# Two chained attention blocks on one core: the loads, transposes and centring of the first microseconds, and the check of the last ones, put in another order

## Chip, cores and metric

The kernel runs on one core of a Trainium2 chip. The metric is the device time of one execution in microseconds (us). An execution computes everything that the reference computes, from inputs in DRAM to the output in DRAM.

## The reference

The input x has the shape (4, 128, 96, 96) in float32: four images of 128 channels and 9216 pixels. Two layers follow each other, each with its own parameters:

```
g     = maxpool2(conv1x1(x, g_w, g_b))      # 64 channels, 48 x 48 = 2304 keys
theta = conv1x1(x, theta_w, theta_b)        # 64 channels, 9216 queries
phi   = maxpool2(conv1x1(x, phi_w, phi_b))  # 64 channels, 2304 keys
attn  = softmax(theta^T phi)                # over the 2304 keys, for each image
y     = attn g^T                            # 64 x 9216
out   = batchnorm(conv1x1(y, W_w, W_b)) + x # 128 x 9216
```

## The kernel before

One image in one layer is a *block*. The eight blocks run in the order of `ORDER`, so that a second layer follows its first with another image between them. The 9216 queries of a block are nine *pairs* of 2 x 512 queries (`Pair`). The 2304 keys are 18 tiles of 128, taken two at a time (`KB`), so a pair has nine steps, and the main loop runs over t = 0 to 647, two key tiles a step.

In a step TensorE makes the scores of two key tiles (`scores`, L351: keys on the partitions, 1024 queries on the free axis, in two buffers of the PSUM pool `ps_sc`), ScalarE turns each into exps (L357, with a constant shift in place of the row maximum), VectorE adds the exps up over the key tiles (`add_up`, L364 and L366) for the denominators, and TensorE multiplies the exps of the step before with the values (`values`, L374). Because the softmax takes a constant shift, notes on the sums and their reciprocals are kept in the tile `notes`. At the end `check` reduces them to one number and `result` writes it as a flag (`flag`). Every engine reads the flag, and `general_blocks`, which takes the true maximum, runs if it says that a sum was too large or too small. For these inputs it does not run.

The order of instructions on TensorE, VectorE, ScalarE and SyncE is written out by hand (`manual_schedule`): each engine takes its instructions in the order of the program text, and a framework places the semaphores. DMAs issued from SyncE (SP) and from ScalarE (ACT) go out in the order of the text too, and one that reuses a semaphore waits for the load that had it before.

The start, before the main loop:

- `load_gphi` loads g's and phi's weights of the first layer (32 KB each), one from ACT's queue and one from SP's. `load_x(0, 12)` loads the first image in 12 loads of 384 KB from SP's queue. `load_theta` loads theta's weights and `columns` four short rows (theta's bias, two variances) from ACT's queue.
- `busy` gives TensorE products of the identity with itself into a tile `warm` (L565, pool `ps_av`): five ahead of the transpose of g's and phi's weights (`make_gphi`, L119) and three behind it.
- `pooled(j)` makes two key tiles: products of x with g's and phi's weights (`products`, L244), and a reduction by VectorE that takes the maximum over 2 x 2 pixels (`pool`, L234). An odd j writes to a buffer of `ps_sc`, an even j to another pool.
- Behind `pooled(0)` come two small transposes, theta's weights (`make_theta`) and the four rows (`first_cols`), each into a buffer of `ps_sc`, and each copied out by VectorE (L121).
- `centring` computes the mean of the first 256 keys, and `batch(j)` has ScalarE subtract it from two key tiles (`centred`, L287) and copy them to the other 64 partitions (`copied`, L293).
- `FIRST` = 6 such batches come ahead of the main loop. The other three are made in its first steps (L208 has their products, in four quadrants of the array). `square` has VectorE transpose the values (L304).

The end: for the last pair `last_denominators` sums the exps by products (L391), takes reciprocals (L399) and has ScalarE sum them up for the notes (L411). `finish` multiplies the values by the reciprocals (L489, four operations of VectorE), makes the last projection (L496), calls `check` (L702 to L708), adds shift and x (L507, four operations), each with its output load (L510), and calls `result` (L712) between the second and the third of them.

Of the kernel before, what the change touches and what calls it, by code (L numbers as in the profile page):

```python
# [9 lines left out]
F32 = mybir.dt.float32  # L10
I32 = mybir.dt.int32
AF = mybir.ActivationFunctionType
ALU = mybir.AluOpType
AX = mybir.AxisListType
PSUM = bass.MemoryType.PSUM

P = 128
# [3 lines left out]
QT = 512  # L21
# [11 lines left out]
PT = 2 * QT  # L33
# [3 lines left out]
FIRST = 6  # L37
# [12 lines left out]
SUM_MIN, SUM_MAX = 1e-20, 1e30  # L50
# [3 lines left out]
def shifted_blocks(ctx: ExitStack, tc: tile.TileContext, x: bass.AP, layers, out: bass.AP, flag):  # L54
# [24 lines left out]
    nc = tc.nc  # L79

    const = ctx.enter_context(tc.tile_pool(name="const", bufs=1))
# [4 lines left out]
    ps_sc = ctx.enter_context(tc.tile_pool(name="ps_sc", bufs=2, space=PSUM))  # L86
# [13 lines left out]
    ones = const.tile([P, CI], F32, name="ones")  # L100
    nc.vector.memset(ones, 1.0)

    notes = const.tile([P, len(ORDER) * NP + 1, 2], F32, name="notes")
    nc.vector.memset(notes, 0.0)

    def load_x(b, n=6):
        xt = xp.tile([C, HW], F32, tag="x", name=f"x_{b}")
        src = x[b].rearrange("c h w -> c (h w)")
        for i in range(n):
            nc.sync.dma_start(out=xt[:, ts(i, HW // n)], in_=src[:, ts(i, HW // n)])  # L110
        return xt
# [86 lines left out]
    def two_banks(name):  # L198
        return [ps_misc.tile([P, QT], F32, tag="misc", name=f"{name}_{i}") for i in range(2)]
# [108 lines left out]
    class Pair:  # L308
# [173 lines left out]
        def finish(self, check, result):  # L482

            n = QT // 2
            y = work.tile([P, PT], F32, tag="halves", name=f"halves_{self.name}")
            for i in range(2):
                for r in range(2):
                    part = slice(r * QT + i * n, r * QT + (i + 1) * n)
                    nc.vector.tensor_mul(y[:, part], self.av[:, part], self.rc[:, ts(i, n)])  # L489
            last = ps_sc.tile([P, PT], F32, tag="sc", name=f"W_ps_{self.name}")  # L490
            pss = [two_banks(f"W_ps_{self.name}"), [last[:, ts(h, QT)] for h in range(2)]]
            for i in range(2):
                for c in range(2):
                    for r in range(2):
                        for h in range(2):
                            nc.tensor.matmul(  # L496
                                pss[i][h][ts(c, CI), :n],
                                lhsT=self.blk.w.W[ts(h, CI), ts(c, CI)],
                                rhs=y[ts(h, CI), r * QT + i * n : r * QT + (i + 1) * n],
                                start=r == 0, stop=r == 1,  # L500
                            )
            good = check()
            for i in range(2):
                for h in range(2):
                    first = (2 * self.p + h) * QT + i * n
                    dst = self.blk.xt[:, first : first + n]
                    nc.vector.scalar_tensor_tensor(  # L507
                        dst, pss[i][h][:, :n], self.blk.w.shift, dst, op0=ALU.add, op1=ALU.add
                    )
                    nc.sync.dma_start(out=self.blk.store[:, first : first + n], in_=dst)  # L510
                if i == 0:
                    result(good)

    def thetas(both):
        pss = two_banks(f"theta_ps_{both[0].name}")
# [12 lines left out]
        return crosswise(part, take)  # L528

    ws = [Layer(l, p) for l, p in enumerate(layers)]  # L530
    ws[0].load_gphi((nc.scalar, nc.sync))
    xs = {0: load_x(0, 12)}
    ws[0].load_theta(nc.scalar)
    first_cols = columns(
        [(ws[0], "theta_b"), (ws[0], "bn_var"), (ws[1], "bn_var")], "first", nc.scalar
    )
# [15 lines left out]
    def begin(n):  # L552

        blocks[n].xt = xs[ORDER[n][0]]
        blocks[n].begin_keys()
# [5 lines left out]
    warm = ps_av.tile([P, PT], F32, tag="av", name="warm_ps")  # L561
# [7 lines left out]
    b0 = blocks[0]  # L569
# [1 line left out]
    ws[0].make_gphi()  # L571
    busy(WARM[1])
    b0.pooled(0)
    ws[0].make_theta(ps_sc.tile([P, PT], F32, tag="sc", name="thetaT_ps")[:, :QT])
    first_cols(ps_sc.tile([P, PT], F32, tag="sc", name="cols_first_ps")[:, :QT])
    b0.centring(KB)
    b0.batch(0)
    for j in range(1, FIRST):
        b0.pooled(j)
        if j == 3:  # L580
            th = ps_sc.tile([P, PT], F32, tag="sc", name="theta_ps_0")[:, :QT]
            pairs[0].theta(th)
            pairs[0].take_theta(th)
        b0.batch(j)
        if j == 1:
            for w in ws:
                w.make_std()
            nc.scalar.preload_act_table(AF.Exp)
# [13 lines left out]
    for n in range(1, len(blocks)):  # L602
        cycle = (n - 1) * NP * NB // CYCLE * CYCLE
        for j in range(NB):
            t = cycle + KEYS[j % len(KEYS)] + j // len(KEYS) * CYCLE
# [13 lines left out]
    for t in range(total + 1):  # L619
        q, s = 2 * (t // CYCLE), t % CYCLE  # L620
        even, odd = pairs[q : q + 2] if t < total else (None, None)
        first, second, take = None, *pending
        pending = (None, None)
        if t in keys:
            n, i = keys[t]
            if n and i == 0:
                begin(n)
            first, *pending = blocks[n].chunks(i)
        elif t < total and s == (THETAS if q else THETAS + 1):
            if q < late:  # L630
                first, *pending = thetas(pairs[q + 1 : q + 3])
            else:
                first, take = odd.theta_alone()
        elif t == total - 1:
            second, take = even.multiply, even.add
        elif gone and s in PROJECT:
            pair = gone[PROJECT.index(s)]
            second, take = pair.multiply, pair.add
        if t < total:
            now, j = divmod(t, NB)  # L640
            if s == 0 and q:
                gone = pairs[q - 2 : q]
            if t in loads:
                xs[loads[t]] = load_x(loads[t])
        for i in range(KB):
            if t < total:
                pairs[now].scores(j * KB + i)
            if i == 0 and first:
                first()
        if second:  # L650
            second()
        for i in range(KB):
            if t < total:
                pairs[now].add_up(j * KB + i)
            if i == 0 and take:
                take()
        if t - 1 in keys and t < NB:
            b0.batch(keys[t - 1][1])
        if t:
            before, j = divmod(t - 1, NB)  # L660
            for k in ends.get(t, range(j * KB, (j + 1) * KB)):
                pairs[before].values(k)
        if t < total:
            for i, pair in enumerate((even, gone[1] if gone else None)):
                if pair is None:
                    continue
                if s in (TURNS[i], TURNS[i] + 1):
                    pair.turn(s - TURNS[i])
                sooner = q == late and i == 0
                if s == (TURNS[0] + 2 if sooner else HALVES[i]):  # L670
                    pair.add_halves()
                if s == (TURNS[0] + 2 if sooner else INVERT[i]):
                    pair.invert()
            for i, pair in enumerate(gone):
                if s == NORM[i]:
                    pair.normalise()
            if q == late and s == 15:
                even.normalise()
        if t == total - 1:
            odd.last_denominators()  # L680
        if t in centres:
            centres[t].centring(KB)
        for i, k in squares.get(t, []):
            b0.square(i, k)
        for k in range(KT // 32):
            if t - k in spreads:
                blk, i = spreads[t - k]
                if k == 0:
                    blk.centred(ts(i, GT * KT))
                if k == 1:  # L690
                    blk.copied(ts(i, GT * KT))
                blk.square(i, k)
        for step in after.pop(t, []):
            step()
    assert not after

    good = const.tile([P, 3], F32, name="good")

    def check():

        ps = ps_sc.tile([P, PT], F32, tag="sc", name="good_ps")[:1, :1]
        nc.vector.tensor_reduce(good[:, 0:1], notes[:, :, 0], AX.X, ALU.add)  # L702
        nc.vector.tensor_scalar(good[:, 1:2], good[:, 0:1], SUM_MAX, None, ALU.is_le)
        nc.vector.tensor_reduce(good[:, 0:1], notes[:, :, 1], AX.X, ALU.add)
        nc.vector.scalar_tensor_tensor(
            good[:, 2:3], good[:, 0:1], 1.0 / SUM_MIN, good[:, 1:2], op0=ALU.is_le, op1=ALU.mult
        )
        nc.tensor.matmul(ps, lhsT=ones[:, :1], rhs=good[:, 2:3], start=True, stop=True)  # L708
        return ps

    def result(ps):
        nc.vector.tensor_scalar(flag, ps, P - 0.5, None, ALU.is_lt)  # L712

    pairs[-1].finish(check, result)

# [303 lines left out]
```

## Time and profile before

| | |
|---|---|
| median of 4 runs | 2496.14 us (2495.37 to 2497.13) |
| profiled execution | 2495.43 us; span from first to last instruction 2493.1 us |
| instructions in the span | 53372 |
| TensorE clock granted, mean | 0.999 |
| busy: TensorE (PE) | 2482.8 us (100% of the span) |
| busy: VectorE (DVE) | 2133.1 us (86%) |
| busy: ScalarE (ACT) | 1542.5 us (62%) |
| exps, L357 | 1296 of 1113 ns |
| sums of exps, L366 | 1151 of 1223 ns |

How to read it: a row of the timeline gives the start in us from the span's start, the time it took, the engine, the line, the operation with the tiles that it writes and reads, and in brackets how long the engine was idle before it and what released it. Equal instructions that follow each other are merged and counted (x8). SPq and ACTq are the instructions by which SyncE and ScalarE issue DMAs. PEld is TensorE's loading of weights, which runs beside its products. A float32 product stands in the trace as two MATMUL records. In the changed kernel the lines stand three to four lower.

### The profile page before, as it was taken

The page shows a single profiled execution, that of the slowest core. Times are in us where ns is not written, and L with a number is a line of the kernel's source. Part 1 is how long each engine was busy: PE and PEld are TensorE (multiplying, and loading weights), DVE is VectorE, ACT ScalarE, POOL GpSimd, SP SyncE. Part 2 cuts the span into 40 slices and gives each one's busy share as a digit, 9 for nine tenths or more (in the row PEclk, how much of TensorE's full clock was granted, in tenths as well). Part 3 has the DMA queues.
Part 4 walks back from the last instruction along what each step waited for, and adds up shares of the span by engine and source line. Part 5 has one row for each costly group of instructions (what it writes and reads, how often), then busy time and mean ns, then how long its engine had stood idle before and what let it go on. Part 6 is the DMA issues. An engine that isn't in the chain of part 4 may idle for free.

```text
span 2493.1 us, 53372 instructions
## 1 busy us (share of the span) xinstructions
PE 2482.8 (100%) x23058; PEld 897.2 (36%) x23058; DVE 2133.1 (86%) x2684; ACT 1542.5 (62%) x1511; POOL 0.7 (0%) x6
## 2 busy tenths in 40 slices
PE   9999999999999999999999999999999999999998
PEld 4333333333333333333333333333333333333333
DVE  7888888888888888888888888888888888888888
ACT  6566666666666666665666566666666566666665
POOL 0000000000000000000000000000000000000000
PEclk9999999999999999999999999999999999999999
DMA  4113111111121222222112112221111221222222
GB/s 157 7 9 86 10 10 10 7 9 10 10 18 23 27 27 19 18 16 75 10 10 18 24 25 27 22 15 10 9 7 9 18 27 23 26 27 26 27 22 41
DMA packets 26888, 60.43 MB, mean 24 GB/s; under 512 B 8330, under 2 KB 9236, under 8 KB 26644
## 3 DMA queue, kind: packets, MB, share of 16 engines
q1 hardware_dynamic: 26476, 56.88, 20.2%
q8 instruction: 182, 2.98, 0.5%
q14 instruction: 62, 0.51, 0.1%
q10 hardware_dynamic: 168, 0.07, 0.0%
HBM read 19.14 MB, written 18.87 MB: 15 GB/s over the span
## 4 chain that ended last, share of the span: by engine, by line


## 5 line engine op out<-in xcount | busy, mean ns | idle before, releaser
L357 ACT ACTIVATE exp<-sc,nshift 128x1024 f32<-128x1024 f32 x1296 | 1386.1, 1113 | 868.7 <-PE sc L351 867.2
L366 DVE TENSOR_TENSOR sum<-sum,exp 128x1024 f32<-128x1024 f32 x1151 | 1407.8, 1223 | 261.3 <-ACT exp L357 214.2
L351 PE MATMUL sc<-theta,phi 64*64 64x512 f32 x10368 | 1248.5, 589 | 0.8 <-ACT exp L357 0.8
L374 PE MATMUL av<-exp,gT 64*64 64x512 f32 x10368 | 1229.6, 589 | 0.0
L374 PEld LDWEIGHTS av<-exp,gT 64*64 64x64 f32 x10368 | 398.8, 133 | 713.3 <-issue 691.8
L351 PEld LDWEIGHTS sc<-theta,phi 64*64 64x64 f32 x10368 | 398.4, 133 | 713.1 <-issue 687.9
L208 PE MATMUL gphi_ps<-x,gphiT 64*64 64x512 f32 x1056 | 137.3, 589 | 0.0
L234 DVE TENSOR_REDUCE gphi<-gphi_ps 128x128 f32<-128x512 f32 x144 | 92.3, 680 | 30.8 <-PE gphi_ps L208 24.6
L364 DVE TENSOR_TENSOR sum<-exp,exp 128x1024 f32<-128x1024 f32 x72 | 88.2, 1225 | 35.5 <-ACT exp L357 34.7
L381 ACT COPY halves<-av 128x1024 f32<-128x1024 f32 x71 | 71.9, 1012 | 50.2 <-PE av L374 50.2
L423 DVE TENSOR_REDUCE parts<-turned 128x16 f32<-128x512 f32 x142 | 97.5, 687 | 4.9
L422 DVE STREAM_TRANSPOSE turned<-sum 128x512 f32<-128x512 f32 x142 | 100.3, 706 | 1.2
L475 DVE SCALAR_TENSOR_TENSOR x<-W_ps,shift,x 128x512 f32<-128x512 f32 x142 | 99.7, 744 | 0.0
L466 PE MATMUL W_ps<-halves,WT 64*64 64x512 f32 x568 | 73.7, 589 | 0.0
L304 DVE STREAM_TRANSPOSE gT<-gphi 32x192 f32<-32x192 f32 x192 | 70.6, 368 | 3.5
L208 PE MATMUL theta_ps<-x,thetaT 64*64 64x512 f32 x560 | 72.8, 589 | 0.0
L208 PEld LDWEIGHTS gphi_ps<-x,gphiT 64*64 64x64 f32 x1056 | 45.2, 132 | 68.1 <-issue 59.2
L435 DVE STREAM_TRANSPOSE four<-parts 32x32 f32<-32x32 f32 x284 | 56.3, 198 | 2.9
L457 DVE TENSOR_TENSOR halves<-halves 128x512 f32<-128x512 f32 x71 | 48.6, 685 | 0.0
L460 DVE TENSOR_TENSOR halves<-halves 128x512 f32<-128x512 f32 x71 | 48.6, 685 | 0.0
L466 PEld LDWEIGHTS W_ps<-halves,WT 64*64 64x64 f32 x568 | 21.7, 133 | 39.2 <-issue 38.7
L208 PEld LDWEIGHTS theta_ps<-x,thetaT 64*64 64x64 f32 x560 | 21.7, 133 | 38.4 <-issue 29.0
(75 smaller groups left out, 216.2 us busy)
## 6 DMA issues: line engine op xcount, KB each, us to landing
halves<-turned SPq DMA_DIRECT2D x142, 128.0 KB
out_dram<-x SPq DMA_DIRECT2D x35, 512.0 KB
x<-in_x_dram SPq DMA_DIRECT2D x18, 768.0 KB
x<-in_x_dram SPq DMA_DIRECT2D x12, 384.0 KB
turned<-both SPq DMA_DIRECT2D x142, 2.0 KB
out_dram<-x SPq DMA_DIRECT2D x4, 128.0 KB
gphi_nat<-in_L_conv_phi_w_dram SPq DMA_DIRECT2D x2, 32.0 KB
rows_other<-in_L_conv_g_b_dram SPq DMA_DIRECT2D x4, 0.2 KB
```

The lines of the kernel that those rows point to most:

```text
L208: nc.tensor.matmul(out, lhsT=lhsT, rhs=rhs, start=step == 0, stop=step == 1)
L234: nc.vector.tensor_reduce(self.gphi[:, ts(k, KT)].rearrange("p (h w) -> p h w", w=w), ps.rearrange("p (h a w b) -> p h w a b", a=2, b=2, w=w),
L351: nc.tensor.matmul(ps[ts(c, CI), ts(h, QT)], lhsT=self.blk.phi[ts(h, CI), ts(2 * k + c, CI)], rhs=self.th[ts(h, CI), :], start=True, stop= ...
L357: nc.scalar.activation(e, ps, AF.Exp, bias=nshift)
L364: nc.vector.tensor_add(self.sum, self.es[0], e)
L366: nc.vector.tensor_add(self.sum, self.sum, e)
L374: nc.tensor.matmul(self.av[ts(h, CI), ts(r, QT)], lhsT=self.blk.gT[ts(r, CI), k, :], rhs=e[ts(r, CI), ts(h, QT)], start=(k == 0), stop=(k ...
L381: nc.scalar.copy(self.halves, self.av)
L422: nc.vector.transpose(self.turned, self.sum[:, ts(h, QT)])
L423: nc.vector.tensor_reduce(self.parts[:, ts(h, QT // SQ)], self.turned.rearrange("p (b k) -> p b k", k=SQ), AX.X, ALU.add,)
L466: nc.tensor.matmul(self.pss[h][ts(c, CI), :], lhsT=self.blk.w.W[ts(h, CI), ts(c, CI)], rhs=self.y[ts(h, CI), :], start=True, stop=True,)
L475: nc.vector.scalar_tensor_tensor(dst, self.pss[h], self.blk.w.shift, dst, op0=ALU.add, op1=ALU.add)
```

## The change

Four things are put in another order:

1. g's and phi's weights of the first layer are both loaded from ACT's queue, so SP's queue begins with x.
2. The two small transposes at the start write to halves of the second bank of the tile `warm` in place of two buffers of `ps_sc`.
3. The last of the six first batches (`batch(5)`) is no longer ahead of the main loop but in its first step, behind the first two exps.
4. `check` is called ahead of the last multiplications and products, and `result` between them and the additions. `check` has one reduction for both notes and one comparison with a tile `limits` (two columns, set at the start), and two products of one column that add up in PSUM, in place of two reductions, two comparisons and one product.

```diff
     notes = const.tile([P, len(ORDER) * NP + 1, 2], F32, name="notes")
     nc.vector.memset(notes, 0.0)
+    limits = const.tile([P, 2], F32, name="limits")
+    for i, limit in enumerate((SUM_MAX, 1.0 / SUM_MIN)):
+        nc.vector.memset(limits[:, i : i + 1], limit)
...
         def finish(self, check, result):
 
             n = QT // 2
+            good = check()
             y = work.tile([P, PT], F32, tag="halves", name=f"halves_{self.name}")
...
-            good = check()
+            result(good)
             for i in range(2):
                 for h in range(2):
...
                     nc.sync.dma_start(out=self.blk.store[:, first : first + n], in_=dst)
-                if i == 0:
-                    result(good)
...
-    ws[0].load_gphi((nc.scalar, nc.sync))
+    ws[0].load_gphi((nc.scalar, nc.scalar))
     xs = {0: load_x(0, 12)}
...
     b0.pooled(0)
-    ws[0].make_theta(ps_sc.tile([P, PT], F32, tag="sc", name="thetaT_ps")[:, :QT])
-    first_cols(ps_sc.tile([P, PT], F32, tag="sc", name="cols_first_ps")[:, :QT])
+    ws[0].make_theta(warm[:, QT : QT + P])
+    first_cols(warm[:, QT + P :])
     b0.centring(KB)
     b0.batch(0)
...
-        b0.batch(j)
+        if j < FIRST - 1:
+            b0.batch(j)
...
+        if t == 0:
+            b0.batch(FIRST - 1)
         if t - 1 in keys and t < NB:
             b0.batch(keys[t - 1][1])
...
-    good = const.tile([P, 3], F32, name="good")
+    good = const.tile([P, 2], F32, name="good")
 
     def check():
 
         ps = ps_sc.tile([P, PT], F32, tag="sc", name="good_ps")[:1, :1]
-        nc.vector.tensor_reduce(good[:, 0:1], notes[:, :, 0], AX.X, ALU.add)
-        nc.vector.tensor_scalar(good[:, 1:2], good[:, 0:1], SUM_MAX, None, ALU.is_le)
-        nc.vector.tensor_reduce(good[:, 0:1], notes[:, :, 1], AX.X, ALU.add)
-        nc.vector.scalar_tensor_tensor(
-            good[:, 2:3], good[:, 0:1], 1.0 / SUM_MIN, good[:, 1:2], op0=ALU.is_le, op1=ALU.mult
-        )
-        nc.tensor.matmul(ps, lhsT=ones[:, :1], rhs=good[:, 2:3], start=True, stop=True)
+        nc.vector.tensor_reduce(good, notes.rearrange("p n w -> p w n"), AX.X, ALU.add)
+        nc.vector.tensor_tensor(good, good, limits, op=ALU.is_le)
+        for i in range(2):
+            nc.tensor.matmul(
+                ps, lhsT=ones[:, :1], rhs=good[:, i : i + 1], start=i == 0, stop=i == 1
+            )
         return ps
 
     def result(ps):
-        nc.vector.tensor_scalar(flag, ps, P - 0.5, None, ALU.is_lt)
+        nc.vector.tensor_scalar(flag, ps, 2 * P - 0.5, None, ALU.is_lt)
```

## The prediction

> **What bounds the kernel now.** I read the page's busy table first, then the timeline of the first 30 us and of the last 10, then who waited for whom on the DMA queue. The page settles what can be won:
>
> ```profile
> PE 2482.8 (100%) x23058; PEld 897.2 (36%) x23058; DVE 2133.1 (86%) x2684; ACT 1542.5 (62%) x1511; POOL 0.7 (0%) x6
> ```
>
> TensorE is busy for 2482.8 of 2493.1 us. The change touches only the first 25 us and the last 10; the stretch from 28.4 to 2476.0 shows 2447.6 us of TensorE in 2447.6 us, and its instructions stay as they are. So the whole play is in the 10.3 us in which TensorE stood idle. 0.2% of this kernel is 5.0 us, about what a measurement of it can tell from no change.
>
> The start, in order of time (start, duration, engine, line, operation, idle before and its releaser):
>
> ```profile
> 0.74 0.58 SPq L135 DMA_DIRECT2D gphi_nat<-in_L_conv_phi_w_dram  x1
> 0.75 0.57 ACTq L135 DMA_DIRECT2D gphi_nat<-in_L_conv_g_w_dram  x1
> 1.35 0.87 ACTq L139 DMA_DIRECT2D theta_nat<-in_L_conv_theta_w_dram  x1
> 1.37 8.33 SPq L110 DMA_DIRECT2D x<-in_x_dram  x12
> 3.65 0.42 PE L119 MATMUL gphiT_ps<-ident,gphi_nat 128*128 128x128 f32 x1
> 3.87 1.11 PE L565 MATMUL warm_ps<-ident 128*128 128x128 f32 x6
> 5.25 2.02 PE L244 MATMUL gphi_ps<-x,gphiT 128*64 128x512 f32 x8 [0.27 <-DMA x<-in_x_dram]
> 7.21 0.27 PE L119 MATMUL thetaT_ps<-ident,theta_nat 64*128 64x64 f32 x1
> 7.33 0.69 DVE L234 TENSOR_REDUCE gphi<-gphi_ps 128x128 f32<-128x512 f32 x1 [0.26 <-PE gphi_ps L244]
> 7.93 0.21 DVE L121 COPY thetaT<-thetaT_ps 128x64 f32<-128x64 f32 x1
> 8.20 5.37 PE L244 MATMUL gphi_ps<-x,gphiT 128*64 128x512 f32 x24 [0.57 <-DVE thetaT L121]
> ```
>
> The weights' transpose at 3.65 starts straight behind five warming products: the weights cost nothing. The first products wait 0.27 us for x, and the next lot 0.57 us for the copy of theta's transpose. Two rows of the queue's waits price a weight load (waiter, what it waited for, total, times, longest):
>
> ```profile
> SPq L110 <- DMA theta_nat<-in_L_conv_theta_w_dram: 2.2, 1, 2.2
> SPq L110 <- DMA gphi_nat<-in_L_conv_phi_w_dram: 0.3, 1, 0.3
> ```
>
> In the queue's timeline the third x load goes out at 2.75, released by phi's weights: landed 2.0 us after their issue at 0.74, with nothing ahead. The fourth goes out at 5.32, released by theta's: 4.0 us after their issue at 1.35, beside an x load of 384 KB. These are the same 32 KB.
>
> Then the first scores:
>
> ```profile
> 19.24 0.50 ACT L287 ACTIVATE phi<-gphi,centre 64x256 f32<-64x256 f32 x1 [1.38 <-DVE gphi L234]
> 20.20 2.12 ACT L357 ACTIVATE exp<-sc,nshift 128x1024 f32<-128x1024 f32 x2
> 21.37 2.09 PE L351 MATMUL sc<-theta,phi 64*64 64x512 f32 x16 [0.77 <-ACT exp L357]
> 25.41 1.28 DVE L234 TENSOR_REDUCE gphi<-gphi_ps 128x128 f32<-128x512 f32 x2
> 26.71 1.11 PE L208 MATMUL gphi_ps<-x,gphiT 64*64 64x512 f32 x8
> ```
>
> and the end:
>
> ```profile
> 2485.57 0.16 DVE L705 SCALAR_TENSOR_TENSOR good<-good 128x1 f32<-128x1 f32 x1
> 2485.65 0.87 DVE L507 SCALAR_TENSOR_TENSOR x<-W_ps,shift,x 128x256 f32<-128x256 f32 x2
> 2486.15 1.79 SPq L510 DMA_DIRECT2D out_dram<-x  x4
> 2486.43 0.13 DVE L712 TENSOR_SCALAR flag<-good_ps 1x1 int32<-1x1 f32 x1
> 2486.50 0.85 DVE L507 SCALAR_TENSOR_TENSOR x<-W_ps,shift,x 128x256 f32<-128x256 f32 x2
> ```
>
> **The change, part by part.** *x ahead of the weights.* SP's x loads start at 0.74 instead of 1.37, 0.63 us sooner. g's weights still go out at 0.75 on ACT's queue, phi's now behind them at about 1.35, theta's at about 1.95, and all beside x. phi's weights then stand exactly where theta's stood: on ACT's queue, issued at 1.35, with an x load ahead. I take theta's row: landed at 5.3. The ends are 1.35 + 2.0 = 3.35 (nothing ahead) and 6.3 (behind two x loads; the second x load was needed at 6.20, 0.95 after the first at 5.25). From landing to first product: about 0.1 for the release, 0.22 from the transpose to the next instruction (3.65 to 3.87), 1.11 for the warming products queued behind it, which are not moved. So the first product starts at 5.3 + 1.43 = 6.73 instead of 5.25: +1.48. x is there by then, so the second pair follows at its pace of 0.86 instead of 0.95: -0.09. With the early end the weights are in time for 3.65 and the first product is held by the warming products to about 5.0: -0.25. With the late end it is +2.4.
>
> The clock: the sixteen warming matmuls have one shape and last 421 ns in the median and 274 at the shortest; the first ten take 2.50 us and the last six 1.11. TensorE gets faster while these run. With the weights late it stands idle from about 4.1 to 5.4 in the middle of that. If it starts slow again, the first products, 1.72 us of them, could take double: up to +1.7 on top. I leave that out of the sum and put it in the range, since most of the warming (3.65 - 1.36 = 2.3 us) has been done by then.
>
> [...]
>
> [...]
>
> Queues moved past: SP's fourth x load now waits for phi's weights (5.3, as it waited for theta's before), the fifth for theta's, one place later; the products need the fifth chunk only 3.4 us after 8.20. The last bn_var row waits on ACT's queue for the first x load (about 4.6); behind it stands only a table load of 1.28 us, and ACT's first work is at 8.88. If the row came over 1 us after the products it would hold the second small transpose.
>
> *Small transposes in the warming tile.* The two transposes no longer hold buffers of the score pool, so the wait of 0.57 us before 8.20 has lost its reason. But both now write one tile, and in the built program the second waits on VectorE's count for the copy of the first. That copy stands behind the reduction that starts at 7.33 and ends at 8.14 either way; the second transpose (0.22 us, before at 7.41 under that reduction) comes after it, and only then the products. The old wait ends at the same copy, so nothing is gained and 0.2 us is added. Bounds: -0.57 if the wait were free, +0.3.
>
> *Last keys centred behind the first exps.* exp 0 no longer waits for the centring at 19.24 (1.38 idle plus 0.93 of work): it starts near 18.95, and TensorE's 0.77 us wait goes. The centring (0.93) then delays exp 2 and 3 by 0.2, and the values need these only from 28.4. What is late next: the products at 26.71 need buffers freed by the reductions of 25.41, which end at 26.69. That chain on VectorE (17.91: two reductions, eight transposes, sum, two transposes, sum, two reductions) is busy throughout and starts from the same products as before; only its sum at 22.35 waited for an exp (ended 22.32), and the transposes ahead of it end at 22.29. So TensorE comes 0.65 earlier and waits again: -0.05, bounds 0 and -0.65.
>
> *Check of sums.* Four small VectorE operations (0.22, 0.15, 0.23, 0.16) become two, about 0.3 and 0.15, ahead of the four multiplications. They can start when ACT's last sum is read (2482.97) and end near 2483.5; the multiplications started at 2483.46: +0.05. Two tiny TensorE products go ahead of products that wait for the multiplications anyway. The additions at 2485.65 started right behind the old check; their products, the first half of the 2.29 us from 2483.94, were done by about 2485.4, so they start near 2485.5, and the last output load goes out 0.15 sooner. The flag is written near 2485.0 instead of 2486.43. The span ends 6.5 us after the old flag: reading it, branching, landing of the outputs. If the outputs decide, the gain is 0.15; if the flag does, 1.4. I take -0.6, as the outputs are still late but the branches start sooner.
>
> *limits* adds two memsets of about 0.06 us near 1.2, when VectorE is idle until 4.11: nothing; 0.1 without that cover.
>
> **Sum.** +1.4 + 0.2 - 0.05 - 0.6 = +0.95, say +1.0. The profiled execution took 2495.43 us (span 2493.1 and 2.3 around it), 0.7 below the median of 2496.14; with +1.0 it would take 2496.4, and the median goes to 2497.1.
>
> **Rivals.** *Weights not held up* (landed by about 3.7): the start costs nothing, 0.2 for the transposes, -0.6 at the end: 2495.6. For it: 32 KB beside 384 KB; against: theta's row. *All as intended*: first products 0.5 sooner, 0.57, 0.77 and up to 1.4 at the end: -3.0, 2493.1. Against it stand the wait on the copy and VectorE's chain. *Weights behind two x loads, or a slow clock*: +2.4 at the start, or +1.4 and up to 1.7: 2498.1 to 2498.8, both 2499.8. *Slower by over 0.2%*: each microsecond that phi's weights land after about 3.9 is a microsecond lost at the start; a loss of 5.0 net of the 0.6 at the end needs them after 9.3 us, behind the fourth x load, which went out at 5.32: 2501.5. The queue's rows show no wait that long.
>
> **Chances.** The forecast 0.55, weights in time 0.20, two loads or slow clock 0.14, all as intended 0.07, over 5 us slower 0.03, over 5 us faster 0.01 (it would take half of all idle time). So faster by over 0.2% 0.01, within 0.96, slower 0.03. The range reaches from weights in time with a good end (2495.2) to most of both, two loads and a slow clock (2499.4).
>
> **What would show it.** Right: the transpose of the weights waits for a DMA, TensorE idle 1 us or more before it; theta's transpose and the second one apart by a VectorE copy; exp 0 before the last centring, and a wait for VectorE's reduction at the products that stood at 26.71; the flag before the last additions. Wrong: the weights' transpose still at 3.65, the products after the small transposes earlier than 8.20, or any change in the 2447.6 us between.

## The result, and the profile after

The changed kernel takes 2499.06 us (median of 32 runs, 2498.17 to 2500.29), the kernel before on the same chip 2496.00 us (52 runs, 2495.03 to 2497.13). The ratio is 1.0012, with a 95% interval of 1.0007 to 1.0017: +3.06 us, below the 5.0 us that counted as a difference here, but real. The forecast was 2497.1 in a range of 2495.2 to 2499.4; the range holds it, and the forecast itself is 2 us too low. The profiled execution took 2498.86 us; its span is 2496.8, 3.7 more than before.

The page's busy row:

```profile
PE 2485.3 (100%) x23060; PEld 901.3 (36%) x23060; DVE 2133.1 (85%) x2684; ACT 1542.7 (62%) x1511; POOL 0.7 (0%) x6
```

TensorE was "busy" 2.5 us more, for two tiny products more. Work cannot account for that: some products must have run slower. The timeline of the start shows which (L113 is SP's x loads, L122 the transposes, L567 the warming products, L247 the products of x):

```profile
0.74 10.42 SPq L113 DMA_DIRECT2D x<-in_x_dram  x12
1.33 0.61 ACTq L138 DMA_DIRECT2D gphi_nat<-in_L_conv_phi_w_dram  x1
5.88 0.45 PE L122 MATMUL gphiT_ps<-ident,gphi_nat 128*128 128x128 f32 x1 [2.02 <-DMA gphi_nat<-in_L_conv_phi_w_dram]
6.11 1.49 PE L567 MATMUL warm_ps<-ident 128*128 128x128 f32 x6
7.53 3.48 PE L247 MATMUL gphi_ps<-x,gphiT 128*64 128x512 f32 x8
10.94 0.27 PE L122 MATMUL warm_ps<-ident,theta_nat 64*128 64x64 f32 x1
11.66 0.21 DVE L124 COPY thetaT<-warm_ps 128x64 f32<-128x64 f32 x1
11.93 0.22 PE L122 MATMUL warm_ps<-ident,rows_first 3*128 3x3 f32 x1 [0.72 <-DVE thetaT L124]
```

and the queue's waits (waiter, what it waited for, total, times, longest):

```profile
SPq L113 <- DMA gphi_nat<-in_L_conv_phi_w_dram: 3.7, 1, 3.7
SPq L113 <- DMA theta_nat<-in_L_conv_theta_w_dram: 0.4, 1, 0.4
```

Phi's weights landed at 5.74: SP, free at 2.0, waited 3.7 us to reuse their semaphore. TensorE was idle for 2.02 us, and then six warming records took 1.49 us, not 1.11, and the first eight products 3.48, not 2.02. The wait for theta's copy that stood ahead of the next products before (0.57) now stands ahead of the second small transpose (0.72).

The first steps of the main loop:

```profile
22.83 1.11 ACT L360 ACTIVATE exp<-sc,nshift 128x1024 f32<-128x1024 f32 x1 [1.09 <-PE sc L354]
25.69 0.51 ACT L290 ACTIVATE phi<-gphi,centre 64x256 f32<-64x256 f32 x1
25.71 1.09 PE L354 MATMUL sc<-theta,phi 64*64 64x512 f32 x8 [0.38 <-ACT exp L360]
29.26 1.28 DVE L237 TENSOR_REDUCE gphi<-gphi_ps 128x128 f32<-128x512 f32 x2
30.06 1.19 PE L211 MATMUL gphi_ps<-x,gphiT 64*64 64x512 f32 x5
30.59 0.14 PEld L211 LDWEIGHTS gphi_ps<-x,gphiT 64*64 64x64 f32 x3 [0.40 <-DVE gphi L237]
31.07 0.60 PE L211 MATMUL gphi_ps<-x,gphiT 64*64 64x512 f32 x3
```

The first scores start at 21.68, 3.88 late. With the centring out of the way TensorE wins 0.54 and stands 3.34 late at 29.20 (before 25.86). Then the products of L211 stop after five records; the other three, at 31.07, stand where 27.22 stood before, 3.85 late: they wait for VectorE's reductions, which are 3.85 late as well (29.26 for 25.41). From there to the last denominators (2481.70 for 2477.85) the distance stays at 3.85. The end:

```profile
2486.86 0.30 DVE L707 TENSOR_REDUCE good<-notes 128x2 f32<-128x146 f32 x1 [0.63 <-ACT theta L414]
2487.20 0.16 DVE L708 TENSOR_TENSOR good<-good,limits 128x2 f32<-128x2 f32 x1
2488.64 0.14 DVE L716 TENSOR_SCALAR flag<-good_ps 1x1 int32<-1x1 f32 x1
2489.25 1.76 DVE L511 SCALAR_TENSOR_TENSOR x<-W_ps,shift,x 128x256 f32<-128x256 f32 x4 [0.47 <-PE W_ps L500]
2489.76 2.81 SPq L514 DMA_DIRECT2D out_dram<-x  x4
```

The additions start 7.55 us behind the last denominators (before 7.79), so 0.24 is won. But the four output issues (SP's instructions that send the outputs out) take 2.81 us together, not 1.79, and from the denominators to the end it is 15.06 us, before 15.22.

### The profile page after: what moved, and what is told of

Its sections match the earlier page's. It is cut to its first block, busy times and chain, and to the rows that moved or that the text cites. A ratio compares the mean times of both kernels' runs of the same rounds, so it can differ in the third digit from the quotient of the medians.

```text
span 2496.8 us, 53373 instructions
## 1 busy us (share of the span) xinstructions
PE 2485.3 (100%) x23060; PEld 901.3 (36%) x23060; DVE 2133.1 (85%) x2684; ACT 1542.7 (62%) x1511; POOL 0.7 (0%) x6
## 4 chain that ended last, share of the span: by engine, by line
PE 99%; DVE 0%; DMA 0%; ACT 0%; ACTq 0%; issue 0%; DVEq 0%
PE sc L354 45%; PE av L377 44%; PE gphi_ps L211 5%; PE W_ps L469 2%; PE theta_ps L211 2%; PE gphi_ps L247 0%; DMA gphi_nat<-in_L_conv_phi_w_dram 0%; DVE sum L402 0%; DVE x L511 0%; PE W_ps L500 0%; PE warm_ps L567 0%; ACT exp L360 0%; PE den_last_ps L394 0%; PE theta_ps L334 0%; PE theta_ps L322 0%; PE gphiT_ps L122 0%
## 5 line engine op out<-in xcount | busy, mean ns | idle before, releaser
L211 PE MATMUL gphi_ps<-x,gphiT 64*64 64x512 f32 x1056 | 139.4, 589 | 0.0
L211 PE MATMUL theta_ps<-x,thetaT 64*64 64x512 f32 x560 | 73.8, 589 | 0.0
L211 PEld LDWEIGHTS gphi_ps<-x,gphiT 64*64 64x64 f32 x1056 | 45.6, 132 | 68.0 <-issue 57.7
L211 PEld LDWEIGHTS theta_ps<-x,thetaT 64*64 64x64 f32 x560 | 21.9, 133 | 38.0 <-issue 28.2
```

Of the source, the lines that this page charges most:

```text
L211: nc.tensor.matmul(out, lhsT=lhsT, rhs=rhs, start=step == 0, stop=step == 1)
```

## The experiments

The theory was that the first part alone makes the loss, twice over: phi's weights land behind the x loads that went out before them, and TensorE's clock falls back in the gap. The rivals were the small transposes, the centring, and the check. All medians are given against the kernel before in the same runs. The interval of each experiment's ratio is some 0.9 per mille to either side, 2.2 us, so the terms of a few tenths are read from the traces, where all instructions of the main loop keep their distance.

| run | median, us | minus before, us | ratio to before, 95% |
|---|---|---|---|
| changed kernel | 2499.06 | +3.06 | 1.0007 to 1.0017 |
| phi's weights first again | 2495.70 | -0.21 | 0.9990 to 1.0008 |
| x first alone | 2499.04 | +3.13 | 1.0004 to 1.0022 |
| 12 warming products ahead, 3 behind | 2497.51 | +1.60 | 0.9996 to 1.0014 |
| 12 warming products ahead, none behind | 2497.16 | +1.25 | 0.9995 to 1.0013 |
| small transposes alone | 2496.58 | +0.41 | 0.9992 to 1.0010 |
| last keys, reductions first | 2495.48 | -0.69 | 0.9989 to 1.0007 |
| check alone | 2495.50 | -0.67 | 0.9989 to 1.0007 |
| all mended | 2494.83 | -1.34 | 0.9985 to 1.0003 |
| theta between x loads | 2498.62 | +2.46 | 1.0002 to 1.0020 |
| phi on POOL's queue | 2499.27 | +3.11 | 1.0003 to 1.0021 |
| mended, flag later | 2495.46 | -0.70 | 0.9989 to 1.0007 |
| half x loads | 2498.97 | +2.84 | 1.0002 to 1.0020 |

**Which part it is.** First the changed kernel with its first part undone:

```diff
-    ws[0].load_gphi((nc.scalar, nc.scalar))
+    ws[0].load_gphi((nc.scalar, nc.sync))
```

> The changed kernel with phi's weights back on SP's queue ahead of x; the other three parts stay. Theory (late weights, and the slow clock behind them, are the whole loss): the transpose of the weights is back at about 3.65 us, the first eight products at 5.25 take 2.0 instead of 3.48. What is left of the change is +0.2 for the wait between the two small transposes, 0 for the centring, -0.15 at the end: 2496.0 + 0.05 = 2496.1. Rival A (the small transposes or the centring cost the time): it stays at 2498 or more. Rival B (the other parts bring what they were meant to, and only the weights hide it): 2493 to 2494.5.

Measured: 2495.70, -0.21. Its timeline:

```profile
3.65 0.42 PE L122 MATMUL gphiT_ps<-ident,gphi_nat 128*128 128x128 f32 x1
5.28 2.04 PE L247 MATMUL gphi_ps<-x,gphiT 128*64 128x512 f32 x8
8.25 0.22 PE L122 MATMUL warm_ps<-ident,rows_first 3*128 3x3 f32 x1 [0.72 <-DVE thetaT L124]
8.39 5.37 PE L247 MATMUL gphi_ps<-x,gphiT 128*64 128x512 f32 x24
```

The start is as before but for the 0.16 us between 5.28 and 8.39 that the small transposes add. Then the same edit by itself, in the kernel before (the diff above, the other way round):

> The kernel before with the one edit that puts phi's weights behind g's on ACT's queue, so that SP begins with x. Theory: the whole of the loss at the start, 3.88 us less 0.2 for the small transposes, 3.7: about 2499.7, a little above the changed kernel, which has 0.15 from its end. Rival A (the loss lies in the other parts): 2496 to 2497. In the trace the theory wants the weights' transpose at about 5.9 and the first eight products at 3.4 us of busy time.

Measured: 2499.04, +3.13, the whole loss; in its trace the weights' transpose stands at 6.04 and the first eight products take 3.58 us:

```profile
6.04 0.45 PE L119 MATMUL gphiT_ps<-ident,gphi_nat 128*128 128x128 f32 x1 [2.17 <-DMA gphi_nat<-in_L_conv_phi_w_dram]
7.70 3.58 PE L244 MATMUL gphi_ps<-x,gphiT 128*64 128x512 f32 x8
```

The forecast for this run was 0.7 too high, because it added the traces' 3.7 to a median.

**The clock or the landing.** Warming products up to the landing, in the changed kernel:

```diff
-WARM = (5, 3)
+WARM = (12, 3)
```

> The changed kernel with twelve warming products ahead of the weights' transpose instead of five, so that TensorE is busy until about 5.6 us (ten records end at 3.9; four more at 0.21 us until the clock rises near 4.45, then ten at 0.11) and not idle from 3.9 to 5.9. The weights land as late as before, at about 5.7. Theory (two losses, late weights and a clock that falls back in the gap): the first eight products take 2.0 us instead of 3.48 and the six warming records ahead of them 0.7 to 1.1 instead of 1.49, so 1.5 to 2.2 us come back: 2496.9 to 2497.6. Rival (the clock is not it; the products are slow because x is still landing): no change, 2499.1. Second rival: the clock rises late whatever runs; twenty-four records at 0.21 us end at 6.5, and the time goes up by about 0.6.

Measured: 2497.51, 1.46 less against the kernel before than the changed kernel's +3.06:

```profile
1.36 5.49 PE L567 MATMUL warm_ps<-ident 128*128 128x128 f32 x24 [1.36 <-POOL ident masks.py:199]
6.64 0.42 PE L122 MATMUL gphiT_ps<-ident,gphi_nat 128*128 128x128 f32 x1
7.93 1.94 PE L247 MATMUL gphi_ps<-x,gphiT 128*64 128x512 f32 x8
```

Both the theory and the second rival had a part of it. The clock did rise late in this run: the 24 records keep their slow distance of 0.213 us to the end (in the kernel before the last warming records, behind the rise at 4.45, are 0.111 apart), and the transpose comes 0.76 later than in the changed kernel. Even so the eight products take 1.94 us, not 3.48, with the same x loads on the way: x did not slow them, the clock did. Then the same without the three products behind:

```diff
-WARM = (5, 3)
+WARM = (12, 0)
```

> As the run before (twelve warming products ahead of the weights' transpose), with no warming products behind it. Theory: the products that use the weights begin as soon as the transpose is copied, about 0.35 us after it, not behind 0.7 to 1.5 us of warming: another 0.4 to 0.9 us below the run with warming behind, 2496.2 to 2497.0. What is then left against the kernel before is the late landing alone (5.7 instead of 3.65, against first products that were held to 5.25 by x). Rival: x or the copy holds the first products as long as the warming did, and nothing is gained.

Measured: 2497.16, 0.35 less than the run with them. The first products wait 0.38 us for VectorE's copy and start at 7.44, not 7.93:

```profile
7.44 1.94 PE L247 MATMUL gphi_ps<-x,gphiT 128*64 128x512 f32 x8 [0.38 <-DVE gphiT L124]
```

That is 0.09 ahead of the changed kernel's 7.53, and they take 1.94 us, not 3.48, so x was there. What is left, +1.25, is the late landing and the 0.75 us by which the warming now holds the transpose (6.63 for 5.88).

Each trace also records when the full clock was granted to TensorE: 4.45 us after the span's start in the kernel before, 10.67 in the changed one. Over all fourteen profiles:

| profiles | idle ahead of the weights' transpose, us | full clock, us after the first product | first eight products, us |
|---|---|---|---|
| nine without a gap | none | 3.08 to 6.15 | 1.94 to 2.76 |
| five with one (changed, x first alone, the three of the next part) | 0.89 to 2.17 | 7.23 to 9.67 | 2.92 to 3.68 |

So, counted from the first product, the time of the grant differs by 3.07 us between the profiles without a gap, and in each of the five with one it came over 1 us after the latest of those.

**What holds phi's weights.** Theta's load goes in between the first two x loads, so that phi's weights have one x load ahead of them:

```diff
         for i in range(n):
+            if b == 0 and i == 1:
+                ws[0].load_theta(nc.sync)
             nc.sync.dma_start(out=xt[:, ts(i, HW // n)], in_=src[:, ts(i, HW // n)])
...
-    ws[0].load_theta(nc.scalar)
```

> The changed kernel with theta's weights moved from ACT's queue to SP's, between the first and the second x load. g's and phi's weights stay on ACT's queue, issued at 0.75 and 1.35; the second x load goes out at about 2.0 instead of 1.37, so phi's weights have one x load ahead of them, not two. Theory (a weight load lands behind every x load that went out before it or with it): phi lands at 4.5 to 5.0 instead of 5.74, the weights' transpose starts about 0.9 earlier, and about 1 us comes back: 2498. Rival (the time from issue to landing is a fixed 4.4 us for a load on a loaded queue): transposed at 5.9 as before, 2499.0. Where the clock rises differs from run to run, so the landing and the transpose decide, more than the time.

Measured: 2498.62, 0.60 less than the changed kernel (against before). Phi's weights landed in sixteen parts, from 4.21 to 5.40 (in the changed kernel from 4.79 to 5.74), and the transpose starts at 5.54, so 0.34 of the 0.9 us came back:

```profile
5.54 0.45 PE L124 MATMUL gphiT_ps<-ident,gphi_nat 128*128 128x128 f32 x1 [1.67 <-DMA gphi_nat<-in_L_conv_phi_w_dram]
```

The theory's direction, not its size. Next, another queue:

```diff
-    ws[0].load_gphi((nc.scalar, nc.scalar))
+    ws[0].load_gphi((nc.scalar, nc.gpsimd))
```

> The changed kernel with phi's weights on POOL's queue instead of behind g's on ACT's; POOL is done with the identity at about 1.3. x stays first on SP's queue. Theory (a weight load lands behind the x loads that went out before it): POOL's issue comes after the second x load's at 1.37, so it helps not at all: landed at 5.5 to 6.5, the time 2499 to 2500. Rival (what held phi's weights was g's load ahead of them on ACT's queue): landed at about 4.2 as g's are now, transposed at 4.3, and the first products, with x there at 3.95 and 5.21, start at 5.8: 2497.

Measured: 2499.27, +3.11. The transpose starts at 5.76, nearly as late as from ACT's queue (5.88), so g's load ahead of phi's was not the cause. TensorE's row shows a side effect: POOL's issue went ahead of the last step of the identity, and the warming waits for it a whole microsecond longer.

```profile
2.37 2.50 PE L567 MATMUL warm_ps<-ident 128*128 128x128 f32 x10 [2.37 <-POOL ident masks.py:199]
5.76 0.47 PE L122 MATMUL gphiT_ps<-ident,gphi_nat 128*128 128x128 f32 x1 [0.89 <-DMA gphi_nat<-in_L_conv_phi_w_dram]
```

Last, the same order with half the bytes in each x load:

```diff
-    xs = {0: load_x(0, 12)}
+    xs = {0: load_x(0, 24)}
```

> The changed kernel with the first block's x loaded in 24 loads of 192 KB instead of 12 of 384 KB; all queues and the order are those of the changed kernel. At 1.35, when phi's weights go out, 384 KB of x are on the way (the second half load goes out at 1.37) instead of 768 KB. Theory (phi's weights land when the x bytes ahead of them have landed): as with one full load ahead, landed at 4.3 to 5.0 instead of 5.74, the weights' transpose about 1 us earlier than 5.88; with the slow clock still there the time falls by 0.9 to 1.4: 2497.7 to 2498.2. Rival (the time depends on how many loads are ahead, or is a fixed 4.4 us): transposed at 5.8, 2499.0, or later, where the smaller loads bring x itself late: twice the issues at 0.6 us each are 15 us for what took 8, so the products of the later chunks may wait.

Measured: 2498.97, but in the trace exactly what the theory said of the landing:

```profile
4.91 0.45 PE L122 MATMUL gphiT_ps<-ident,gphi_nat 128*128 128x128 f32 x1 [1.05 <-DMA gphi_nat<-in_L_conv_phi_w_dram]
```

Landed at 4.77, transpose 0.97 earlier. So the bytes of x ahead of the weights count here: landed at 5.74 behind 768 KB, at 4.77 behind 384 KB. They are not all: in the run with theta's load between, 384 KB of x went out ahead too (with theta's 32 KB), and phi's weights landed at 5.40. In these three expectations the second x load stands at 1.37; that is its time in the kernel before. With x first it goes out at 1.19, or 1.20 with phi on POOL's queue, and in the POOL and the half-load run it is ahead of phi's load. Why the time did not follow is open: in the profile TensorE reaches the last denominators 1.5 us sooner than in the changed kernel (2480.19), but the end behind them took 15.96 us.

**The small transposes by themselves**, in the kernel before:

```diff
-    ws[0].make_theta(ps_sc.tile([P, PT], F32, tag="sc", name="thetaT_ps")[:, :QT])
-    first_cols(ps_sc.tile([P, PT], F32, tag="sc", name="cols_first_ps")[:, :QT])
+    ws[0].make_theta(warm[:, QT : QT + P])
+    first_cols(warm[:, QT + P :])
```

> The kernel before with the one edit that puts the two small transposes into the warming tile. Theory (both now write one tile, so the second waits for VectorE's copy of the first, and the products stand behind it): the 24 products that began at 8.20 us begin 0.2 later, at 8.40, if the first products begin at 5.25; 2495.9 + 0.2 = 2496.1. Rival (the edit frees the score buffers, and the wait of 0.57 us goes): they begin at 7.6, and the time falls to 2495.3.

Measured: 2496.58, +0.41.

```profile
5.30 2.76 PE L244 MATMUL gphi_ps<-x,gphiT 128*64 128x512 f32 x8
7.99 0.27 PE L119 MATMUL warm_ps<-ident,theta_nat 64*128 64x64 f32 x1
8.98 0.22 PE L119 MATMUL warm_ps<-ident,rows_first 3*128 3x3 f32 x1 [0.71 <-DVE thetaT L121]
9.13 5.37 PE L244 MATMUL gphi_ps<-x,gphiT 128*64 128x512 f32 x24
```

The 24 products start at 9.13, 0.93 late, but 0.78 of that was there before the transposes (7.99 for 7.21): in this run the clock rose only at 7.00, in the middle of the first products. The edit itself costs 0.15; nothing was won.

**The last keys, with the reductions ahead.** In the kernel before, the third part, and in the second step the reductions ahead of the sum:

```diff
+        if t == 0:
+            b0.batch(FIRST - 1)
...
         for i in range(KB):
+            if i == 0 and take and t == 1:
+                take()
             if t < total:
                 pairs[now].add_up(j * KB + i)
-            if i == 0 and take:
+            if i == 0 and take and t != 1:
                 take()
```

> The kernel before with the centring of the last keys behind the first exps, and one more edit: in the second step VectorE's reductions of the products of the keys go ahead of the sum of exps instead of behind it, so they start at about 24.3 instead of 25.4 us. Theory (the 0.5 to 0.65 us that the centring wins on TensorE are lost again in the changed kernel only because the products there wait for these reductions): now they are kept, TensorE is 0.5 to 0.65 ahead of the kernel before at 32 us and at its end, 2495.9 - 0.6 = 2495.3. Rival (something else takes them back, the exps or the values' wait for the centring): TensorE is level with the kernel before by 32 us, 2495.9.

Measured: 2495.48, -0.69. The timeline:

```profile
24.18 1.24 DVE L234 TENSOR_REDUCE gphi<-gphi_ps 128x128 f32<-128x512 f32 x2
25.45 2.55 DVE L366 TENSOR_TENSOR sum<-sum,exp 128x1024 f32<-128x1024 f32 x2
26.21 1.04 PE L208 MATMUL gphi_ps<-x,gphiT 64*64 64x512 f32 x8
```

The products run as one group of eight at 26.21, 0.50 ahead of the kernel before, and do not stop; the last denominators come at 2477.40, 0.45 ahead. The run with phi's weights first again has the same move of the last keys without the reductions ahead: there TensorE stands 0.35 ahead at 25.51, the products stop after five, and from the sixth on (27.39 for 27.22) to the last denominators it is 0.17 behind. So in the changed kernel VectorE's order is what takes the half microsecond back.

**The check by itself**, in the kernel before (the fourth part's diff):

> The kernel before with the check of sums ahead of the last multiplications and the flag ahead of the last additions, nothing else. Theory (the last outputs decide the end, and only the additions' 0.25 us count): 2495.9 - 0.2 = 2495.7. Rival (the flag, read by the engines before they branch, decides): it is written 1.6 us sooner, and the time falls by 0.6 to 1.4: 2494.5 to 2495.3. From the old flag to the end of the span it was 6.5 us; the theory wants 8 us or so from the new one.

Measured: 2495.50, -0.67, between the theory's time and the rival's; but in its profile the end behind the denominators is 15.32 us, no shorter than before. The output issues are long again:

```profile
2486.17 2.93 SPq L514 DMA_DIRECT2D out_dram<-x  x4
```

**All mended.** Phi's weights first, and

```diff
     ws[0].make_theta(warm[:, QT : QT + P])
-    first_cols(warm[:, QT + P :])
+    first_cols(ps_sc.tile([P, PT], F32, tag="sc", name="cols_first_ps")[:, :QT])
```

so that no transpose waits for the other's copy, and the reductions ahead as above:

> The version that should beat both: weights ahead of x as in the kernel before; theta's transpose in the warming tile but the second small transpose in a score buffer, so that it waits for no copy and the next products find a free buffer; the last keys centred behind the first exps with the reductions ahead of the sum; the check ahead of the last products. Theory, step by step: -0.57 at the products that began at 8.20, -0.6 from the centring kept, -0.2 at the end, -1.4 in all: 2494.5. Rival (the gains hide one another, each a wait for VectorE that the next one takes over): 2495.3 to 2495.9.

Measured: 2494.83, -1.34: the fastest version, though its interval still touches 1.

```profile
7.79 0.27 PE L122 MATMUL warm_ps<-ident,theta_nat 64*128 64x64 f32 x1
8.00 0.22 PE L122 MATMUL cols_first_ps<-ident,rows_first 3*128 3x3 f32 x1
8.15 5.58 PE L247 MATMUL gphi_ps<-x,gphiT 128*64 128x512 f32 x24
10.04 0.23 PEld L247 LDWEIGHTS gphi_ps<-x,gphiT 128*64 128x64 f32 x4 [0.84 <-DVE centre L285]
13.53 1.06 PE L322 MATMUL theta_ps<-x,thetaT 128*64 128x512 f32 x4
2485.55 3.55 SPq L514 DMA_DIRECT2D out_dram<-x  x4
```

From theta's transpose to the 24 products it is 0.36 us, 0.99 before. Not all of this is kept: the 24 products take 5.58 us, not 5.37, with one more wait for VectorE at 10.04, so that theta's products, which follow, win 0.45 (13.53, 5.74 behind the transpose; before 13.40, 6.19 behind it). With the 0.5 of the last keys, TensorE gains 0.94 from theta's transpose to the last denominators (2477.49), though the late clock had cost it 0.58 before. The output issues take 3.55. To see why, the flag alone was moved back between the additions:

```diff
-            result(good)
             for i in range(2):
                 for h in range(2):
...
                     nc.sync.dma_start(out=self.blk.store[:, first : first + n], in_=dst)
+                if i == 0:
+                    result(good)
```

> The mended version (weights first, second small transpose in a score buffer, reductions ahead of the sum, check ahead of the last products) with only the flag's write moved back between the last additions, where the kernel before has it. Theory (the early flag lets the engines branch while the outputs are going out; their code loads, 16 KB each, hold an engine of the DMA for 1.2 to 1.7 us, and the third or fourth output issue takes 1.2 to 1.9 us instead of 0.44; that is why the 0.25 us of the additions never reach the end): all four issues take 0.33 to 0.45, and from the last denominators to the end it is about 15.1 us instead of 16.0 in the mended version's profile: 0.2 to 0.5 faster than 2494.8. Rival (the issue is long for another reason): the third or fourth issue stays over 1 us, and the time is the same or, with the flag later, up to 1 us longer.

Measured: 2495.46, by the medians 0.6 slower than with the early flag, which the intervals do not tell apart, though the issues are short:

```profile
2485.14 1.80 SPq L513 DMA_DIRECT2D out_dram<-x  x4
```

The first half of the theory stands: with the early flag an output issue is long, with the later one none is, in all nine profiles with the early flag (2.8 to 3.6 us for the four issues) and all five with the later one (1.79 to 1.80). The second half fell: the end got no shorter (16.28 us behind the denominators, 16.03 with the early flag).

## Why the prediction was right, and where it was short

The sign was right, and so was the cause, late weights and a wait of TensorE for them. The size was not: +1.0 forecast, +3.06 measured. That the range holds it is owed to its upper part, which the rival "two loads or a slow clock" (chance 0.14) had brought in; what happened is some of both.

*Late weights.* The landing was mis-sized: phi's weights were put at 5.3, by theta's row, and landed at 5.74, about halfway to the other bound (6.3, two loads ahead). Theta's row was read with an x load ahead of it; theta's load went out at 1.35 and the x load beside it at 1.37. In the changed kernel two x loads go out ahead of phi's at 1.33, the first at 0.74 and

```profile
1.19 0.42 SPq L113 DMA_DIRECT2D x<-in_x_dram  x1
```

and in the run with half loads, with 384 KB ahead in place of 768, the weights landed at 4.77. The transpose came 0.48 later than forecast.

*The clock* is the term that was mis-sized: taken at nothing, with up to +1.7 in the range. It cost 0.32 in the warming behind the transpose (1.65 us from the transpose to the first product, forecast 1.33) and 1.54 in the first products (3.41 from the first to theta's transpose, forecast 1.87): 1.86. The reason given, that most of the warming had been done, did not hold: with 2.5 us of products ahead of the gap, the full clock still came 4.8 us after the products went on, against 3.08 us after the first product in the kernel before. Nor could its time be foreseen from one profile: without a gap it came 3.08 to 6.15 us after the first product. The 1.7 that the prediction kept for the range was nearer than its nothing in the sum.

Together: +1.4 was forecast up to theta's transpose, +3.73 measured (10.94 for 7.21); 0.48 and 1.86 make up the difference. With +0.15 for the small transposes, -0.03 for the last keys and -0.17 at the end this is the 3.68 by which the two spans differ. In the medians the first part is worth +3.13, less than in that one profile. A likely reason, not shown for the kernel's own other runs, is that it pays for a late clock as well: in the six other profiles that start with phi's weights first, theta's transpose comes at 7.25 to 7.99, not 7.21. The profiled execution of before had the clock up at 4.45, the earliest of all, and lay 0.7 below its median; I carried that 0.7 over without asking what it was.

The prediction's early end, 3.35 with nothing ahead of the weights, was further off than theta's row (5.3): they landed at 5.74 from ACT's queue and at about 5.7 from POOL's.

*Small transposes.* +0.2 forecast; 1.14 us from theta's transpose to the 24 products against 0.99, so +0.15, by the wait on the copy that was named.

*Last keys.* -0.05 forecast, -0.03 measured: 0.54 won and lost again at the products behind the reductions, where it was said to be lost.

*Check.* -0.6 forecast, between -0.15 and -1.4; the profiles do not show it. The additions came 0.24 sooner, forecast 0.15. The end behind the denominators took 15.06 us for 15.22, and over all profiles 14.99 to 16.05 in the nine with the early flag, 15.21 to 16.28 in the five with the later one. The median of the check alone is 0.67 less, inside its interval of 2.2. What took the place of the gain in the profiles had not been foreseen: the flag is written 1.64 us sooner against the denominators (2488.64, ahead of the output issues from 2489.76), so the engines, which branch on it, can do so while the outputs go out. A code load of 16 KB then starts in the middle of the output issues (2490.46, for 1.19 us), and the third issue, from 2490.64, ends at 2491.83, just behind it. In the kernel before the same code load starts at 2488.47, after the last issue. With phi's weights first again it starts at 2487.44, in the fourth issue, and there the fourth is the long one (1.47 us). That the code load is what holds the issue is read from these times; that the flag's place decides it, the run with the flag later shows. How much of the 0.6 there is stays unsettled, since the end differs by 1 us between profiles with the same instructions there.

## What to carry to other kernels

A small load that everything waits for goes ahead of the big ones: here phi's weights landed 3.4 to 4.6 us after their issue with 384 or 768 KB of x ahead of them, 2.0 us with none, and POOL's queue in place of ACT's brought them no sooner (about 5.7 for 5.74). An idle gap in TensorE's first microseconds was paid twice here, once as the gap (2.02 us) and once as slow products behind it (1.86 us), and filling it with warming products brought back 1.46 us, 1.81 without the three behind the transpose. So a gap that cannot be closed is worth filling, but not beyond its end: the twelve warming products held the transpose 0.75 us longer than the late weights had. When a wait is taken away, look on the waiting engine for the next wait that ends at the same engine; the move of the last keys won nothing (-0.03) until VectorE's reductions went one place earlier too (0.45 at the last denominators).

## What the runs showed of the hardware that was not expected

- The full clock was granted at another time in each profile, though the products of those named here started at 1.36: without a gap 3.1 us after that (before), 3.3 (last keys), 3.9 (phi's weights first again), 5.6 (small transposes alone), 6.2 (twelve warming products). Behind the gap of 2.0 us it came 4.8 us after the products went on.
- The shortest gap, 0.89 us (phi on POOL's queue, where the warming also began 1.0 us later), went with the slowest first eight products, 3.68 us; in the nine profiles without a gap they took 1.94 to 2.76.
- Two things that differ from profile to profile are of the size of the kernel's own spread of 2 us: theta's transpose came 0.78 later with the late clock of the transposes' run, and the end differs by 1 us. That they make up the spread is not shown.
- A 32 KB load issued at 1.33 landed at 5.74 behind 768 KB of x, at 4.77 behind 384 KB. From another engine's queue, issued at 1.27 behind 768 KB, it landed 4.4 us later, at about 5.7, and released the transpose at 5.76.
- Four output issues took 1.79 to 1.80 us in the five profiles with the later flag, and 2.8 to 3.6 in the nine with the early one. The long issue is in each of the nine the one beside the first 16 KB code load: the third in eight, the fourth in one.
